# Feed-forward of a decoder layer: four fp32 matmuls per chunk become eight float32r matmuls on a split input

## The chip, the cores and the metric

The kernel runs on one core of one Trainium2 chip. A core has TensorE (PE, with its weight loads shown apart as PEld), VectorE (DVE), ScalarE (ACT), GpSimd (POOL) and SyncE (SP, which issues the DMAs here). The metric is device time in microseconds, the median over runs. A "pass" below is one record of a matmul in the trace: one stream of columns through the array.

## The reference

One decoder layer over x of shape (2, 2048, 512), in fp32, with three residual blocks:

```python
x = x + attn(layernorm(x), Wq, Wk, Wv, Wo)      # 16 heads of 32, rotary positions, softmax over 2048 keys
x = x + gelu(layernorm(x) @ ctx.T) @ ctx        # ctx: 77 rows of 512
w = (weights >= 0.0) * 2.0 - 1.0                # signs, 512 x 512
x = x + clip((layernorm(x) @ w.T) * scale + bias, -100, 100)
```

The change concerns the third block: its weights are only +1 and -1, and its input is a normalised chunk of 128 rows.

## The kernel before, in words

**Stages.** For each of the two batches, `project_batch` normalises 16 chunks of 128 rows, turns them and makes queries, keys and values; then `Attention.run` goes through 32 units (a block of queries, a group of four heads, a half of 256 queries) of 8 steps each. A step treats 2 x 128 keys for four heads; it has two half-steps, one for each pair of heads. In a half-step TensorE makes scores (`st`, L496, and at times the row maxima's start, L481), the products from which later row maxima are taken (`ps`, L403), the weighted values of the step before (`acc`, L514) and sums of weights (L528); ScalarE takes exponentials (`pw`, L623), VectorE reduces `ps` to maxima (`mx`, L415), GpSimd adds weights up (`sm`, L625).

**The rest of the layer in the gaps.** When all heads of a block of queries are done, `divide` appends `after_attention` for that block to `queue`. It is a generator of small pieces: the output projection (`po`, L309), a layernorm, the two matmuls with ctx (`ph`, L316, and `po`, L335), a layernorm, and the feed-forward (`pf`, L343) with scale, bias, clip and residual, for each chunk of 128 rows. `background(1)` runs one piece of the first generator in the queue. Each `yield` says whether the next piece is heavy (it has matmuls): in the second half-step of every step any piece may run, in the first half-step of every second step only a light one; in the last four units of a batch each half-step may take any piece.

**Order.** Inside `run` the order on PE, DVE, ACT and POOL is that of the program (`tc.manual_schedule`); outside it the framework schedules. Pieces that are left when a batch ends go into the next batch's projection or, after the second batch, into a loop at the end in which `side()` moves the element-wise work from GpSimd to VectorE.

**Buffers.** While attention runs, `bank` gives the background its PSUM banks from `ps_s`, which has three; the `ps` products use two of them in each half-step. Tiles with the tag "w" in `work` (five buffers) hold `xn2`, `h`, `u`, `y` and `num`. The pool `big` has three buffers with the tag "s", which hold `r` in the projection and `pw` in attention.

**The lines around the change.** `norm` (L291) makes `xn2` on ScalarE (L297), transposes it on TensorE into `pt2` (L303; the trace calls it `pt`) and copies it with ScalarE into `ot` (L304), which is the block's own part of the query tile (`q` in the trace). After the layernorm of all n chunks of a block, a loop (L340 to L353) makes, for each chunk, the matmuls

```python
nc.tensor.matmul(pf, ot[:, i, cols], wf[:, i, :], start=(i == 0), stop=(i == ND - 1))
```

and `nc.vector.tensor_mul(y, pf, fs)` (L345); then, a piece each, the addition of the bias (L347), and clip and residual (L349, L350) with the DMA to the output (L352). `late_loads` loads the weights `wf` after the first projection's code and turns them into signs in place (L111, L112).

Of the kernel before, what the change touches and what calls it, by code (L numbers as in the profile page):

```python
# [8 lines left out]

F32 = mybir.dt.float32  # L10
BF16 = mybir.dt.bfloat16
AF = mybir.ActivationFunctionType
ALU = mybir.AluOpType
AX = mybir.AxisListType

P = 128
B, S, D = 2, 2048, 512
H, DK = 16, 32
C = 77
ND = D // P  # L20
BLK = 512
# [9 lines left out]
MAX_VAL = 100.0  # L31
# [4 lines left out]
def decoder_layer(  # L36
# [16 lines left out]
    nc = tc.nc  # L53

    const = ctx.enter_context(tc.tile_pool(name="const", bufs=1))
    kvq = ctx.enter_context(tc.tile_pool(name="kvq", bufs=1))
    xpool = ctx.enter_context(tc.tile_pool(name="xpool", bufs=6))
    big = ctx.enter_context(tc.tile_pool(name="big", bufs=3))
    sums = ctx.enter_context(tc.tile_pool(name="sums", bufs=3))
    work = ctx.enter_context(tc.tile_pool(name="work", bufs=5))  # L60
# [6 lines left out]
    def load_x(b, ch):  # L67
        t = xpool.tile([P, D], F32, tag="x", name=f"x_{b}_{ch}")
        nc.sync.dma_start(t, x[b, ch * P : (ch + 1) * P, :])
        return t  # L70

    def load_w(src, name):
        t = const.tile([P, ND, D], F32, tag=name, name=name)
        nc.sync.dma_start(t, src.rearrange("(i p) o -> p i o", p=P))
        return t


    def load_qkv():
        return [load_w(w, name) for w, name in ((wk_t, "wk"), (wq_t, "wq"), (wv_t, "wv"))]

    x_next = [load_x(0, 0), load_x(0, 1)]
    qkv = load_qkv()
    cos = const.tile([P, NCH, DK // 2], F32, tag="cos", name="cos")
    sin = const.tile([P, NCH, DK // 2], F32, tag="sin", name="sin")
    nc.sync.dma_start(cos, rope_cos.rearrange("(c p) d -> p c d", p=P))
    nc.sync.dma_start(sin, rope_sin.rearrange("(c p) d -> p c d", p=P))

    ident = const.tile([P, P], F32, tag="ident", name="ident")
    make_identity(nc, ident)
    ident_b = const.tile([P, P], BF16, tag="ident_b", name="ident_b")  # L90
    nc.vector.tensor_copy(ident_b, ident)
    ones_b = const.tile([P, P], BF16, tag="ones_b", name="ones_b")
    nc.vector.memset(ones_b, 1.0)
    ones = const.tile([P, DK], F32, tag="ones", name="ones")
    nc.vector.memset(ones, 1.0)
# [5 lines left out]
    for n in range(2):  # L101
        mt = const.tile([P, 2, 4, DK], BF16, tag=f"mt{n}", name=f"mt{n}")
        nc.vector.memset(mt, 0.0)
# [3 lines left out]

    def late_loads():
        late["wo"] = load_w(wo_t, "wo")
        wf = load_w(wf_t, "wf")  # L110
        nc.vector.tensor_scalar(wf, wf, 0.0, 2.0, ALU.is_ge, ALU.mult)  # L111
        nc.vector.tensor_scalar_add(wf, wf, -1.0)  # L112
        late["wf"] = wf
        for name, src in (("fs", f_scale), ("fb", f_bias)):
            t = const.tile([P, D], F32, tag=name, name=name)
            nc.sync.dma_start(t, src.to_broadcast([P, D]))
            late[name] = t
# [9 lines left out]
    def chunk_stats(xc, mv):  # L127
        st = small.tile([P, 6], F32, tag="st", name="st")
        nc.vector.bn_stats(st, xc)
        nc.vector.bn_aggr(mv, st)  # L130


    def scale_and_shift(engine, mv, n):
        y = small.tile([P, n], F32, tag=f"rstd{n}", name="rstd")
        engine.tensor_scalar(y, mv[:, :, 1], EPS, None, ALU.add)
        nc.gpsimd.tensor_tensor(y, y, minus_half[:, :n], ALU.pow)
        off = small.tile([P, n], F32, tag=f"off{n}", name="off")
        engine.tensor_mul(off, mv[:, :, 0], y)
        engine.tensor_scalar(off, off, -1.0, None, ALU.mult)
        return y, off  # L140
# [116 lines left out]
    def side():  # L257
        return nc.vector if alone else nc.gpsimd
# [5 lines left out]
    def bank(shape, name):  # L264
        banks[0] += 1
        if attending or (alone and banks[0] % 2):
            return ps_s.tile(shape, F32, tag="s", name=name)
        return ps_t.tile(shape, F32, tag="t", name=name)


    def after_attention(b, blk, ot, first, end):
        wo, wf, fs, fb = late["wo"], late["wf"], late["fs"], late["fb"]
        ctxn, ctxt = late["ctx"]
        n = end - first
        chunks = [slice(c * P, (c + 1) * P) for c in range(first, end)]
        whole = slice(first * P, end * P)
        xs = [load_x(b, blk * CPB + c) for c in range(first, end)]
        yield True


        def add_to_x(matmuls, mv):
            for c in range(n):
                ps = bank([P, D], "po")
                matmuls(ps, chunks[c])
                nc.vector.tensor_add(xs[c], ps, xs[c])
                yield False
                chunk_stats(xs[c], mv[:, c, :])
                yield c + 1 < n


        def norm(mv):  # L291
            y, off = scale_and_shift(side(), mv, n)
            yield False
            yield False
            for c in range(n):
                xn = work.tile([P, D], F32, tag="w", name="xn2")
                nc.scalar.activation(  # L297
                    xn, xs[c], AF.Identity, bias=off[:, c : c + 1], scale=y[:, c : c + 1]
                )
                yield True  # L300
                pt = bank([P, ND, P], "pt2")
                for i in range(ND):
                    nc.tensor.transpose(pt[:, i, :], xn[:, i * P : (i + 1) * P], ident)  # L303
                nc.scalar.copy(ot[:, :, chunks[c]], pt)  # L304
                yield c + 1 == n

        def project_out(ps, cols):
            for i in range(ND):
                nc.tensor.matmul(ps, ot[:, i, cols], wo[:, i, :], start=(i == 0), stop=(i == ND - 1))  # L309

        mv = small.tile([P, n, 2], F32, tag=f"mv{n}", name="mv2")
        yield from add_to_x(project_out, mv)
        yield from norm(mv)
        ph = bank([C, n * P], "ph")
        for i in range(ND):
            nc.tensor.matmul(ph, ctxt[:, i, :], ot[:, i, whole], start=(i == 0), stop=(i == ND - 1))  # L316
        h = work.tile([C, n * P], F32, tag="w", name="h")
        nc.scalar.copy(h, ph)
        yield False
        u = work.tile([C, n * P], F32, tag="w", name="u")  # L320
        side().tensor_mul(u, h, h)
        yield False
        side().tensor_scalar(u, u, 0.044715, 1.0, ALU.mult, ALU.add)
        side().tensor_mul(u, u, h)
        yield False
        yield False
        nc.scalar.activation(u, u, AF.Tanh, scale=GELU_C)
        yield False
        side().tensor_scalar(u, u, 1.0, 0.5, ALU.add, ALU.mult)
        side().tensor_mul(u, u, h)  # L330
        yield False
        yield True

        def attend_ctx(ps, cols):
            nc.tensor.matmul(ps, u[:, cols.start - whole.start : cols.stop - whole.start], ctxn, start=True, stop=True)  # L335

        mv = small.tile([P, n, 2], F32, tag=f"mv{n}", name="mv3")
        yield from add_to_x(attend_ctx, mv)
        yield from norm(mv)
        for c, cols in enumerate(chunks):  # L340
            pf = bank([P, D], "pf")
            for i in range(ND):
                nc.tensor.matmul(pf, ot[:, i, cols], wf[:, i, :], start=(i == 0), stop=(i == ND - 1))  # L343
            y = work.tile([P, D], F32, tag="w", name="y")
            nc.vector.tensor_mul(y, pf, fs)  # L345
            yield False
            side().tensor_add(y, y, fb)  # L347
            yield False
            side().tensor_scalar(y, y, -MAX_VAL, MAX_VAL, ALU.max, ALU.min)  # L349
            side().tensor_add(xs[c], xs[c], y)  # L350
            r0 = blk * BLK + (first + c) * P
            nc.sync.dma_start(out[b, r0 : r0 + P, :], xs[c])  # L352
            yield True  # L353

# [20 lines left out]
    class Attention:  # L377
# [53 lines left out]
        def turn_maxima(self, u):  # L431
            mt = mts[u % 2]
            mrow = small.tile([P, 2, P], BF16, tag="mrow", name="mrow")
            if u > 0:
                nc.sync.dma_start_transpose(mrow, mt.rearrange("p c h d -> p (c h d)"))
            else:
                pt = ps_s.tile([P, 2, P], BF16, tag="s", name="ptm")
                for c in range(2):
# [213 lines left out]
    for b in range(B):  # L652
        att = Attention(b)
        project_batch(b, x_next, att, *qkv)
        if b == 0:
            late_loads()
        load_ctx(b)
        att.run()
        if b + 1 < B:
            x_next = [load_x(b + 1, 0), load_x(b + 1, 1)]  # L660
            qkv = load_qkv()
# [51 lines left out]
```

## Time and profile before

| | us |
|---|---|
| median of 3 runs (lowest, highest) | 2783.71 (2783.66, 2784.01) |
| the profiled execution's own time | 2784.56 |
| its span, from first to last instruction | 2782.8 |
| PE busy | 2750.7 (99%) |
| PEld, weight loads, overlapping PE | 1491.3 (54%) |
| POOL busy | 1756.4 (63%) |
| DVE busy | 1675.7 (60%) |
| ACT busy | 1320.4 (47%) |
| mean granted TensorE clock | 0.996 |

Busy times overlap between engines. A PE that is busy all the time is not at its peak, since ends of matmuls are modelled; start times are what can be relied on. In the groups of instructions, the numbers after the bar are busy us in total and mean ns of one, then idle time of the engine just before them with what ended it. In the timeline, the first two columns are start and length in us.

### The profile page before, as it was taken

The page shows a single profiled execution, that of the slowest core. Times are in us where ns is not written, and L with a number is a line of the kernel's source. Part 1 is how long each engine was busy: PE and PEld are TensorE (multiplying, and loading weights), DVE is VectorE, ACT ScalarE, POOL GpSimd, SP SyncE. Part 2 cuts the span into 40 slices and gives each one's busy share as a digit, 9 for nine tenths or more (in the row PEclk, how much of TensorE's full clock was granted, in tenths as well). Part 3 has the DMA queues.
Part 4 walks back from the last instruction along what each step waited for, and adds up shares of the span by engine and source line. Part 5 has one row for each costly group of instructions (what it writes and reads, how often), then busy time and mean ns, then how long its engine had stood idle before and what let it go on. Part 6 is the DMA issues. An engine that isn't in the chain of part 4 may idle for free.

```text
span 2782.8 us, 70154 instructions
## 1 busy us (share of the span) xinstructions
PE 2750.7 (99%) x30748; PEld 1491.3 (54%) x30748; DVE 1675.7 (60%) x2792; ACT 1320.4 (47%) x2391; POOL 1756.4 (63%) x1903
## 2 busy tenths in 40 slices
PE   8999999999999999999999999999999999999997
PEld 4445555555555555555444455555555555555554
DVE  3436777676666666665234367766757666666652
ACT  2114555455545554654321155555555455545552
POOL 3226767567756685777542277766777567756764
PEclk9999999999999999999999999999999999999999
DMA  4000000000000000000210000000000000000000
GB/s 141 19 16 2 5 4 4 4 4 19 19 4 4 10 27 3 4 19 18 69 31 27 15 4 4 4 4 4 4 24 14 4 4 15 22 3 4 22 7 16
DMA packets 41858, 43.52 MB, mean 16 GB/s; under 512 B 24758, under 2 KB 24758, under 8 KB 41552
## 3 DMA queue, kind: packets, MB, share of 16 engines
q1 hardware_dynamic: 41552, 39.05, 4.7%
q8 instruction: 240, 3.93, 0.6%
q14 instruction: 66, 0.54, 0.1%
HBM read 26.58 MB, written 8.39 MB: 13 GB/s over the span
## 4 chain that ended last, share of the span: by engine, by line
PE 97%; POOL 1%; DVE 1%; DMA 0%; ACT 0%; issue 0%; ACTq 0%; POOLq 0%; DVEq 0%
PE st L496 22%; PE acc L514 22%; PE ps L403 18%; PE acc L528 8%; PE po L309 4%; PE pf L343 4%; PE pq L168 4%; PE pk L168 4%; PE pv L168 4%; PE st L481 3%; PE pt L303 1%; PE po L335 1%; PE ph L316 1%; PE ptqk L176 1%; PE pt L161 1%
## 5 line engine op out<-in xcount | busy, mean ns | idle before, releaser
L625 POOL TENSOR_TENSOR sm<-pw 128x512 f32<-128x512 f32 x1024 | 1296.6, 1271 | 634.5 <-ACT pw L623 631.8
L415 DVE TENSOR_REDUCE mx<-ps 128x1 f32<-128x512 f32 x2048 | 1310.3, 681 | 582.0 <-PE ps L403 579.5
L623 ACT ACTIVATE pw<-st 128x512 f32<-128x512 f32 x2048 | 1111.8, 595 | 1001.8 <-PE ps L403 668.8
L403 PE MATMUL ps<-k,q 32*128 32x512 f32 x4096 | 1208.8, 640 | 1.6 <-DVE mx L415 1.6
L514 PE MATMUL acc<-pw,v 128*32 128x256 f32 x8192 | 655.6, 391 | 0.0
L528 PE MATMUL acc<-sm,ones 128*32 128x128 f32 x7680 | 389.0, 280 | 0.0
L403 PEld LDWEIGHTS ps<-k,q 32*128 32x128 f32 x4096 | 355.3, 183 | 37.7 <-issue 25.8
L514 PEld LDWEIGHTS acc<-pw,v 128*32 128x32 f32 x8192 | 162.4, 108 | 396.3 <-issue 376.6
L528 PEld LDWEIGHTS acc<-sm,ones 128*32 128x32 f32 x7680 | 247.4, 110 | 153.9
L496 PE MATMUL st<-q,dkk 32*128 32x256 f32 x2048 | 291.1, 400 | 0.0
L496 PE MATMUL st<-q,dkq 32*128 32x256 f32 x2048 | 289.9, 400 | 0.0
L496 PE MATMUL st<-q,dkv 32*128 32x256 f32 x2048 | 289.9, 400 | 0.0
L496 PE MATMUL st<-q,k 32*128 32x256 f32 x2048 | 262.8, 374 | 0.0
L201 POOL TENSOR_TENSOR r<-r 128x512 f32<-128x512 f32 x64 | 82.1, 1282 | 246.6 <-DVE r L200 246.3
L496 PEld LDWEIGHTS st<-q,dkk 32*128 32x128 f32 x2048 | 175.4, 184 | 93.2 <-issue 52.3
L496 PEld LDWEIGHTS st<-q,dkq 32*128 32x128 f32 x2048 | 172.7, 184 | 82.6 <-issue 56.7
L496 PEld LDWEIGHTS st<-q,dkv 32*128 32x128 f32 x2048 | 174.7, 184 | 65.2 <-issue 33.6
L496 PEld LDWEIGHTS st<-q,k 32*128 32x128 f32 x2048 | 195.2, 187 | 14.2
L548 DVE RECIPROCAL num<-num 128x128 f32<-128x128 f32 x128 | 120.2, 941 | 60.8 <-ACT num L542 60.8
L177 ACT COPY q<-ptqk 128x512 f32<-128x512 f32 x32 | 18.8, 587 | 232.5 <-PE ptqk L176 232.5
L168 PE MATMUL pk<-wk,xnt 128*128 128x512 f32 x256 | 120.7, 615 | 2.7 <-ACT xnt L163 2.7
L168 PE MATMUL pq<-wq,xnt 128*128 128x512 f32 x256 | 120.9, 612 | 0.0
(90 smaller groups left out, 1860.7 us busy)
## 6 DMA issues: line engine op xcount, KB each, us to landing
x<-in_x_dram SPq DMA_DIRECT2D x64, 256.0 KB, 2.7
out_dram<-x SPq DMA_DIRECT2D x32, 256.0 KB, 2.0
wk<-in_wk_t_dram SPq DMA_DIRECT2D x2, 1024.0 KB, 5.5
wq<-in_wq_t_dram SPq DMA_DIRECT2D x2, 1024.0 KB, 10.5
wv<-in_wv_t_dram SPq DMA_DIRECT2D x2, 1024.0 KB, 9.7
wo<-in_wo_t_dram SPq DMA_DIRECT2D x1, 1024.0 KB
wf<-in_wf_t_dram SPq DMA_DIRECT2D x1, 1024.0 KB, 9.8
mrow<-mt SPq DMA_TRANSPOSE x62, 2.3
```

The source lines that it names most:

```text
L168: nc.tensor.matmul(dst, xnt[:, i, :], w[:, i, :], start=(i == 0), stop=(i == ND - 1))
L309: nc.tensor.matmul(ps, ot[:, i, cols], wo[:, i, :], start=(i == 0), stop=(i == ND - 1))
L343: nc.tensor.matmul(pf, ot[:, i, cols], wf[:, i, :], start=(i == 0), stop=(i == ND - 1))
L403: nc.tensor.matmul(ps, self.q[qb][self.rows[h], g, q0 : q0 + P], self.k[kb][self.rows[h], g, :], start=True, stop=True,)
L415: nc.vector.tensor_reduce(mx[:, qc, h, kb : kb + 1], ps, AX.X, ALU.max)
L481: nc.tensor.matmul(self.st[h], ones_b[r, :], mrow[r, None, :].to_broadcast([DK, 2, HQ]), start=True, stop=False, skip_group_check=True,)
L496: nc.tensor.matmul(self.st[h][:, c, :], keys[r, g, kc * P : (kc + 1) * P], self.q[qb][r, g, hf * HQ : (hf + 1) * HQ], start=False, stop=Tr ...
L514: nc.tensor.matmul(acc[self.rows[h], 0, :], self.v[self.chunk(i, c)][:, d0 : d0 + DK], pw[:, h, c, :], start=(i == 0 and c == 0), stop=(i ...
L528: nc.tensor.matmul(acc[self.rows[h], 1, part], ones, sm[:, h, part], start=False, stop=(i == STEPS - 1), skip_group_check=True,)
L548: nc.vector.reciprocal(num[:, 1, part], num[:, 1, part])
L623: nc.scalar.activation(pw[:, h], self.st[h], AF.Exp, scale=SCALE)
L625: nc.gpsimd.tensor_add(sm[:, hs, :], pw[:, hs, 0, :], pw[:, hs, 1, :])
```

## The change

The feed-forward's matmuls are made in float32r, a 4-byte type with a shorter mantissa; as the change has it, such a matmul is one pass where an fp32 one is two. The signs are exact in it. The normalised, transposed chunk is split into two parts: `high` is `pt2` written as float32r (ScalarE[...]), `low` is `pt2 - high` (VectorE). Four matmuls with `high` and four with `low` are accumulated in `pf`. The feed-forward of a chunk now follows its own transposes, in `norm`, by the argument `take`, in place of a loop after all chunks; the number of pieces, and of heavy ones, is the same. `ot` is not written by the second layernorm any more. The weights are loaded into a buffer of `big`, and their signs written into a float32r tile.

```diff
 def late_loads():
     late["wo"] = load_w(wo_t, "wo")
-    wf = load_w(wf_t, "wf")
-    nc.vector.tensor_scalar(wf, wf, 0.0, 2.0, ALU.is_ge, ALU.mult)
-    nc.vector.tensor_scalar_add(wf, wf, -1.0)
+    drawn = big.tile([P, ND, D], F32, tag="s", name="wf")
+    nc.sync.dma_start(drawn, wf_t.rearrange("(i p) o -> p i o", p=P))
+    nc.vector.tensor_scalar(drawn, drawn, 0.0, 2.0, ALU.is_ge, ALU.mult)
+    wf = const.tile([P, ND, D], F32R, tag="wf", name="signs")
+    nc.vector.tensor_scalar_add(wf, drawn, -1.0)
     late["wf"] = wf
...
-        def norm(mv):
+        def norm(mv, take):
...
-                nc.scalar.copy(ot[:, :, chunks[c]], pt)
-                yield c + 1 == n
+                yield from take(c, pt)
+
+        def keep(c, pt):
+            nc.scalar.copy(ot[:, :, chunks[c]], pt)
+            yield c + 1 == n
+
+        def feed_forward(c, pt):
+            parts = [work.tile([P, ND, P], F32R, tag="w", name=name) for name in ("high", "low")]
+            nc.scalar.copy(parts[0], pt)
+            nc.vector.tensor_sub(parts[1], pt, parts[0])
+            yield True
+            pf = bank([P, D], "pf")
+            for k, part in enumerate(parts):
+                for i in range(ND):
+                    nc.tensor.matmul(
+                        pf,
+                        part[:, i, :],
+                        wf[:, i, :],
+                        start=(k == 0 and i == 0),
+                        stop=(k == 1 and i == ND - 1),
+                    )
+            y = work.tile([P, D], F32, tag="w", name="y")
+            nc.vector.tensor_mul(y, pf, fs)
+            yield False
+            side().tensor_add(y, y, fb)
+            yield False
+            side().tensor_scalar(y, y, -MAX_VAL, MAX_VAL, ALU.max, ALU.min)
+            side().tensor_add(xs[c], xs[c], y)
+            r0 = blk * BLK + (first + c) * P
+            nc.sync.dma_start(out[b, r0 : r0 + P, :], xs[c])
+            yield False
...
-        yield from norm(mv)
+        yield from norm(mv, keep)
...
-        yield from norm(mv)
-        for c, cols in enumerate(chunks):
-            pf = bank([P, D], "pf")
-            for i in range(ND):
-                nc.tensor.matmul(pf, ot[:, i, cols], wf[:, i, :], start=(i == 0), stop=(i == ND - 1))
-            y = work.tile([P, D], F32, tag="w", name="y")
-            nc.vector.tensor_mul(y, pf, fs)
-            yield False
-            side().tensor_add(y, y, fb)
-            yield False
-            side().tensor_scalar(y, y, -MAX_VAL, MAX_VAL, ALU.max, ALU.min)
-            side().tensor_add(xs[c], xs[c], y)
-            r0 = blk * BLK + (first + c) * P
-            nc.sync.dma_start(out[b, r0 : r0 + P, :], xs[c])
-            yield True
+        yield from norm(mv, feed_forward)
```

## The prediction

> **What bounds the kernel now.** I read the page's busy times and its chain of waits first.
>
> ```profile
> PE 2750.7 (99%) x30748; PEld 1491.3 (54%) x30748; DVE 1675.7 (60%) x2792; ACT 1320.4 (47%) x2391; POOL 1756.4 (63%) x1903
> ...
> PE 97%; POOL 1%; DVE 1%; DMA 0%; ACT 0%; issue 0%; ACTq 0%; POOLq 0%; DVEq 0%
> PE st L496 22%; PE acc L514 22%; PE ps L403 18%; PE acc L528 8%; PE po L309 4%; PE pf L343 4%; PE pq L168 4%; PE pk L168 4%; PE pv L168 4%; PE st L481 3%; PE pt L303 1%; PE po L335 1%; PE ph L316 1%; PE ptqk L176 1%; PE pt L161 1%
> ```
>
> The end is set by TensorE nearly throughout, and `pf`, the line that changes, holds 4% of the chain. Since a busy PE need not be a bound, I then looked in the timeline at start times around one `pf`:
>
> ```profile
> 664.15 0.64 PE L514 MATMUL acc<-pw,v 128*32 128x256 f32 x8
> ...
> 664.93 3.70 PE L343 MATMUL pf<-wf,q 128*128 128x512 f32 x8
> ...
> 669.63 0.64 PE L514 MATMUL acc<-pw,v 128*32 128x256 f32 x8
> ...
> 671.53 0.64 PE L514 MATMUL acc<-pw,v 128*32 128x256 f32 x8
> ```
>
> From L514 to L514 is one half-step: 5.48 us with `pf`, 1.90 us without. So `pf` costs 3.6 us of progress, its full length on PE, and nothing else hides it. Half-steps without `ps` (the last units) take 1.85, those with it 1.86 to 1.90: PE's own stream sets the pace, VectorE's maxima are just short of it. The groups by shape give the durations:
>
> ```profile
> L343 PE MATMUL pf<-wf,q 128*128 128x512 f32 x256 | 119.8, 612 | 0.0
> L349 POOL TENSOR_SCALAR y<-y 128x512 f32<-128x512 f32 x30 | 57.6, 1921 | 0.2
> L285 DVE TENSOR_TENSOR x<-po,x 128x512 f32<-128x512 f32 x64 | 43.7, 685 | 102.8 <-PE po L309 89.6 <-PE po L335 13.2
> L304 ACT COPY q<-pt 128x512 f32<-128x512 f32 x64 | 37.5, 586 | 13.9 <-PE pt L303 13.2
> L303 PEld LDWEIGHTS pt<-ident,xn 128*128 128x128 f32 x256 | 27.5, 143 | 27.0 <-ACT xn L297 12.1 <-ACT pw L623 7.8 <-issue 7.1
> ```
>
> 256 records for 32 x 4 matmuls: two passes each. The chain has eight passes of 512 columns in 3.43 us in the projection, 0.429 each; in attention a group costs 3.60, so 0.17 is the price of changing over, which stays.
>
> **What the Trainium skill says.** "Perfetto Trace Analysis", Engine Utilization: the array gives 307.2 G elements/s, half of it for FP32_LOW_HIGH. For 128 x 512 that is 0.213 and 0.427 us; the trace's fp32 pass, 0.429, is the halved one. "FP8 and Floating Point Precision", TensorE Precision Notes: the array is natively about FP22, "FP32 reduced precision" reads 4 bytes and truncates to FP22, and true fp32 takes four passes. The trace shows two passes of half rate, which is the same time. No rate is stated for the reduced form. "TensorE: Matmul & The Clock Gate", Wait — 56ns, not 53.3ns?: a warm pass of 512 columns measures 0.2157 us. The one kind here that isn't fp32 agrees: `st` by L481 in bf16, 512 columns, is followed on the same rows after 0.23 us.
>
> ```profile
> 637.94 0.39 PE L481 MATMUL st<-mrow,ones_b 32*128 32x512 bf16 x2
> ...
> 638.17 0.59 PE L496 MATMUL st<-q,k 32*128 32x256 f32 x4
> ```
>
> **The change, part by part.**
>
> The passes. Per chunk, 8 x 0.429 = 3.43 us go; 8 float32r passes of 512 columns come, and no float32r is in the trace. Lower bound 0.2157 (the rate of a non-fp32 pass), upper 0.429 (4-byte data at fp32's rate). I take 0.2157: the halving is named for the two-part form alone, and a one-part operand leaves no reason for it. Weight loads of 4-byte data, 128 x 128, must then fit under 0.2157: the transposes, a load and a 128-column pass each, run four in 0.59 us, 0.147 apart, so loads at that pace fit. Gain: 8 x (0.429 − 0.2157) = 1.706 us a chunk.
>
> Where the chunks are. The compiled order keeps all 28 chunks inside attention, two in the second batch's projection and two in the last loop, and the last `pf` of each block falls in the same half-step as before; `pf` follows its transposes by two half-steps (one in the last units). 28 x 1.706 = −47.8. In the projection PE is bound as well: 2 x 1.706 = −3.4.
>
> The last loop. PE has been idle and is cold: the skill's clock page ("What's actually happening") gives half clock after an idle window, and the trace shows the first eight passes there taking 5.3 us (2768.4 to 2773.7), the next eight 3.4, so cold lasts to about 2772.1. With short passes: `high` is there at 2768.2, eight cold passes (0.43 each) end at 2771.7, then one cold and seven warm at 2773.7. On DVE `low` (0.69, twice) lies under this; after the second `pf` its chain of 0.69 + 0.69 + 0.43 + 0.69, mixed with one addition of the first chunk, ends near 2777.1, before 2779.8: −2.5.
>
> The split. ScalarE's copy to `high` replaces the copy to `ot`, 0.586 for 0.586: 0. `tensor_sub` is new on DVE, nearest row L285 (PSUM and SBUF in, 128x512), 0.685 x 32 = 21.9 us busy, DVE at 60%. Behind it on DVE stand the reductions of the next half-step, and for these PE waits by its three PSUM banks. The copy ends 2.07 us after the L514 of the half-step of the transposes (2.45 to 2.56 long), so the subtraction lies from 2.1 to 2.8, 0.3 us into the next, where reductions are due at 0.1. The trace has the like: BATCH_NORM_STATS2 (0.69) at 597.64 pushes the reductions from 0.10 to 0.23 and that half-step takes 1.99 instead of 1.90; where they are pushed to 0.45 it takes 2.21. Bounds 0.1 and 0.31; I take 0.18 x 28 = +5.0. `pf` itself does not wait: it comes at least a half-step later.
>
> GpSimd. Bias, clip and residual (1.27 + 1.92 + 1.27 = 4.46) are the same work, spread over chunks, but less PE time covers them. In the last units the cycle becomes five half-steps: 5 x 1.9 + 0.59 + 1.9 = 12.0 us, in which POOL has 5 x 1.27 + 4.46 plus about 0.6 of `divide` and maxima = 11.4. Before: three half-steps with `pf`, 9.3 us against 8.7. After a clip, `sm` lags 3.2 to 3.5 us already now (4.5 once) and PE doesn't wait; the sums are used about two half-steps later. I take +1.5 in all, from 0 to 10.
>
> The signs. `drawn` takes the buffer of `r` of chunk 13, free when its transposes end at 201.6; on SP it comes behind x loads already issued by 189.3. 1 MB lands 5.5 to 9.8 us later (times of L74), 207 to 211.4. On DVE it stands between two copies of keys with 2.7 us idle (208.5 to 211.2), before `ps` reductions at 213.2. Between 0 and +4; I take +1.0. On SP the maxima's transposes behind it aren't due until later units. The two operations' cover in the first chunks falls away, 2.4 us that nobody waited for.
>
> Other edits (two `take` functions, `keep`) change no instruction: 0. "w" gets two more tiles per chunk, but their readers end before five more are taken: 0.
>
> Sum: −47.8 − 3.4 − 2.5 + 5.0 + 1.5 + 1.0 = −46.2. The profiled execution's 2784.6 (span 2782.8 and 1.8 around it) would become 2738.4; the median is 0.85 below that execution, so 2737.5.
>
> **The rivals.**
>
> R1, half rate: float32r streams at fp32's 0.429 because of its four bytes. For it: every 4-byte matmul in the trace has this rate, and no page states another. Against it: the name in the halving rule. Then the passes gain nothing and the additions remain: 2783.7 + 5.0 + 1.5 + 1.0 + 0.7 (`low` in the last loop) = 2792, slower. It decides from a pass of about 0.40 us upwards, where 30 x 8 x (0.429 − p) equals the 7.5 of costs.
>
> R2, weight loads not hidden: the array can't start a load under so short a pass, and pass plus load make 0.30 (0.2157 and the part of 0.147 that is left). For it: PEld rows show 0.19 for these loads; against it: the loads of `pf` now idle 0.24 between, so they run ahead. Gain 30 x 8 x 0.129 = 31, time 2783.7 − 31 − 2 + 7.5 = 2758.
>
> R3, another engine takes over around `pf`: GpSimd's 11.4 of 12.0, or the reductions with the subtraction ahead of them. If each of 28 chunks loses 0.5 us more, 2751.5. Against it: the lags above that cost nothing.
>
> **How the numbers follow.** Chances: forecast 0.76, R1 0.11, R2 0.06, R3 0.07. With its bounds (subtraction −2 to +4, signs −1 to +3, GpSimd −1.5 to +8, not all at once) the forecast's own range is 2729 to 2747. R3 and half of R2 reach to 2757; so 2727 to 2757 leaves R1, the rest of R2 and the forecast's edges out, 0.2. A measurement tells 0.2%, 5.6 us, from no change: faster 0.89 (forecast, R2, R3), slower 0.08 and same 0.03 (R1, whose 2792 has the bound at 2789.3 below it).
>
> **What would show it.** Right: `pf` with 256 records in float32r, eight of them in about 1.73 us by starts, a half-step with `pf` at 3.8 us instead of 5.5; the half-step after the transposes 0.1 to 0.3 longer; span near 2736. Wrong: starts 0.43 apart (R1), 0.3 (R2), PE idle before L528 by `sm` or L403 by `mx` (R3); a stall near 208 to 214 by `drawn`. More than two records per pair of parts and slice would make the change itself untrue.

## The result

The changed kernel takes 2735.1 us (median of 4 runs, 2733.57 to 2737.15) against 2783.7 before: a ratio of 0.9827, 95% interval 0.9813 to 0.9841. The forecast was 2737.5, range 2727 to 2757. On a third chip, later, it took 2736.4 against 2783.9, ratio 0.9831 (0.9818 to 0.9844). The total is close to the forecast; its terms are less so, and two misses of 4 to 5 us stand against each other, as the next sections show.

The page of the changed kernel, busy times and the chain of waits:

```profile
PE 2700.9 (99%) x30748; PEld 1493.1 (55%) x30748; DVE 1695.3 (62%) x2824; ACT 1321.0 (48%) x2391; POOL 1755.2 (64%) x1903
...
PE 98%; DVE 1%; POOL 0%; ACT 0%; issue 0%; DMA 0%; ACTq 0%; POOLq 0%
PE st L516 22%; PE acc L534 22%; PE ps L423 18%; PE acc L548 8%; PE po L343 4%; PE pq L171 4%; PE pk L171 4%; PE pv L171 4%; PE st L501 3%; PE pf L323 2%; PE pt L306 1%; PE po L369 1%; PE ph L350 1%; PE ptqk L179 1%; PE pt L164 1%
```

The bound is where it was. PE is busy 49.8 us less with as many records (30748: per chunk, two for each of four matmuls before, one for each of eight now), and `pf` went from 4% of the chain to 2%. VectorE has 32 instructions and 20 us more.

The timeline around one `pf` of the changed kernel, and its groups by shape (count, then busy us and mean ns, then idle time before):

```profile
640.58 0.64 PE L534 MATMUL acc<-pw,v 128*32 128x256 f32 x8
...
641.36 1.19 PE L323 MATMUL pf<-signs,high 128*128 128x512 f32 x4
...
642.39 1.09 PE L323 MATMUL pf<-signs,low 128*128 128x512 f32 x4
...
644.49 0.64 PE L534 MATMUL acc<-pw,v 128*32 128x256 f32 x8
```

```profile
L323 PE MATMUL pf<-signs,high 128*128 128x512 f32 x128 | 39.4, 431 | 0.1
L323 PE MATMUL pf<-signs,low 128*128 128x512 f32 x128 | 36.0, 403 | 0.0
...
L318 DVE TENSOR_TENSOR low<-pt,high 128x512 fp32r<-128x512 f32 x32 | 22.0, 687 | 48.2 <-ACT high L317 48.2
...
L317 ACT CAST high<-pt 128x512 fp32r<-128x512 f32 x32 | 18.8, 586 | 14.6 <-PE pt L306 14.6
```

From L534 to L534 a half-step with `pf` is now 3.91 us where it was 5.48. Its passes start 0.23 us apart, not 0.429 and not the 0.2157 of the forecast: from the first start to what follows `pf` it is 2.06 us in each of the 28 groups of attention within 0.02, against 3.63. The mean durations of 431 and 403 ns would mislead here, since the records overlap: they start 0.23 us apart and are 0.39 us long or more. The split costs what it was costed at on its engines, 0.687 and 0.586 us.

Where the 49.2 us between the two profiled executions (spans of 2782.8 and 2733.6) went, by stages cut at the first and last weighted-value matmuls of each batch:

| stage | before, us | after, us | difference |
|---|---|---|---|
| first projection, to the first L514 or L534 | 228.26 | 229.68 | +1.42 |
| attention of batch 0 | 1133.44 | 1112.20 | −21.24 |
| second projection | 249.51 | 242.67 | −6.84 |
| attention of batch 1 | 1132.39 | 1111.13 | −21.25 |
| last loop | 39.20 | 37.90 | −1.29 |

Only the two attention stages repeat: in a second profile of the changed kernel (r1_changed below) they are 1112.25 and 1111.31, while its first projection is 231.9 and its last loop 35.1. What moves the other stages is taken up below.

### The profile page after: what moved, and what is told of

Read it like the earlier page. It is cut to its first block, busy times and chain, and to the rows that moved or that the text cites. A ratio compares the mean times of both kernels' runs of the same rounds, so it can differ in the third digit from the quotient of the medians.

```text
span 2733.6 us, 70216 instructions
## 1 busy us (share of the span) xinstructions
PE 2700.9 (99%) x30748; PEld 1493.1 (55%) x30748; DVE 1695.3 (62%) x2824; ACT 1321.0 (48%) x2391; POOL 1755.2 (64%) x1903
## 4 chain that ended last, share of the span: by engine, by line
PE 98%; DVE 1%; POOL 0%; ACT 0%; issue 0%; DMA 0%; ACTq 0%; POOLq 0%
PE st L516 22%; PE acc L534 22%; PE ps L423 18%; PE acc L548 8%; PE po L343 4%; PE pq L171 4%; PE pk L171 4%; PE pv L171 4%; PE st L501 3%; PE pf L323 2%; PE pt L306 1%; PE po L369 1%; PE ph L350 1%; PE ptqk L179 1%; PE pt L164 1%
## 5 line engine op out<-in xcount | busy, mean ns | idle before, releaser
L534 PE MATMUL acc<-pw,v 128*32 128x256 f32 x8192 | 655.6, 391 | 0.0
L534 PEld LDWEIGHTS acc<-pw,v 128*32 128x32 f32 x8192 | 162.5, 108 | 396.9 <-issue 378.6
```

The source lines that it names most:

```text
L534: nc.tensor.matmul(acc[self.rows[h], 0, :], self.v[self.chunk(i, c)][:, d0 : d0 + DK], pw[:, h, c, :], start=(i == 0 and c == 0), stop=(i ...
```

## The experiments

Two theories stood from the start. T: the gain is the shorter pass of float32r and little else. O: the new order, feed-forward right behind each chunk's transposes, carries a good part of it. The two misses to be explained were the pass (0.232 for 0.2157) and the subtraction (free, where the forecast had 5 us). e1 to e4 ran on a second chip, where the kernel before takes 2783.1 us; the others on the third, where it takes 2783.9.

**e1_order_fp32: the order alone.**

```diff
-            parts = [work.tile([P, ND, P], F32R, tag="w", name=name) for name in ("high", "low")]
+            parts = [work.tile([P, ND, P], F32, tag="w", name="whole")]
             nc.scalar.copy(parts[0], pt)
-            nc.vector.tensor_sub(parts[1], pt, parts[0])
```

(and the signs loaded and made as in the kernel before; `stop` goes to the last matmul that is left, here and in e2)

> The order of the changed kernel (feed-forward of each chunk right after its transposes), but fp32: no split, four two-pass matmuls, signs made in place early. Theory (the gain is the shorter pass): a pf group costs 3.63 us again, attention takes 1133.4 us per batch as before, the first L514-type matmul starts at 228.3 us as before, and only the stall in the second batch's projection can go, 2 to 5 us: 2779 to 2782 us. Rival (the order itself carries a good part of the gain, by spreading the work over half-steps): 2770 us or less. Rival (the projection's stall comes from the length of the passes, not from their place): 2783.7 us.

Measured: 2782.9 us, ratio to before 0.9999 (0.9991 to 1.0007). The timeline of this kernel:

```profile
639.17 0.64 PE L531 MATMUL acc<-pw,v 128*32 128x256 f32 x8
...
639.96 3.70 PE L320 MATMUL pf<-wf,whole 128*128 128x512 f32 x8
...
644.66 0.64 PE L531 MATMUL acc<-pw,v 128*32 128x256 f32 x8
```

A half-step with `pf` is 5.49 us again. O falls: the order is worth nothing in the median. The median is 0.9 us above the theory's range and 0.8 below the second rival, while single executions reach from 2779.8 to 2786.1, so it does not decide between these two. Attention is 1134.24 and 1133.18 us, 0.8 longer per batch than before: some half-steps with moved pieces are 0.1 longer. In the profiled execution the second projection was 242.8 us, as short as the changed kernel's, and yet the median has no gain. So that part of the difference comes and goes with the execution; the section on the hardware says with what.

**e2_high_only: half of the passes, no subtraction.**

```diff
-            parts = [work.tile([P, ND, P], F32R, tag="w", name=name) for name in ("high", "low")]
+            parts = [work.tile([P, ND, P], F32R, tag="w", name="high")]
             nc.scalar.copy(parts[0], pt)
-            nc.vector.tensor_sub(parts[1], pt, parts[0])
```

> Leaves out the low part: no subtraction on VectorE, four float32r passes per chunk in place of eight. Theory (a pass costs 0.232 us of progress, the subtraction about 0.05): 28 x (0.93 + 0.05) + 2 x 0.93 + about 1 at the end = 30 us less than the changed kernel, about 2705 us. Rival (a group has a large fixed cost, so half of the passes save less): 2715 us or more. Rival (the subtraction costs the 0.18 of the forecast): 2701 us.

Measured, with the low part's products left out: 2706.7 us, ratio 0.9727 (0.9714 to 0.9740), as the theory had it within 2 us. Its executions reach from 2702.3 to 2709.7, so the median rules out the large fixed cost but not the 2701 of the last rival; the stages do that. A group is 1.13 us long in place of 2.06, so four passes are 0.93 and a fixed 0.20 is left. Attention of batch 0 is 1099.68, 12.5 us less than in the changed kernel; the passes alone make 14 x 0.93 = 13.0. With 0.18 for each subtraction it would be 15.5. Nothing is left for the subtraction.

**e3_cols256: the same columns in twice as many passes and weight loads.**

```diff
-            for k, part in enumerate(parts):
-                for i in range(ND):
-                    nc.tensor.matmul(pf, part[:, i, :], wf[:, i, :], ...)
+            for o in (slice(0, D // 2), slice(D // 2, D)):
+                for k, part in enumerate(parts):
+                    for i in range(ND):
+                        nc.tensor.matmul(pf[:, o], part[:, i, :], wf[:, i, o], ...)
```

> Each float32r matmul cut in two of 256 columns: sixteen passes and sixteen weight loads per chunk, same product. Theory A (a pass is its columns at 2.4 per ns plus about 19 ns): 16 x (0.107 + 0.019) + 0.1 = 2.1 us per group, about 2735 to 2737 us in all. Theory B (0.232 us is the pace of loading 128 x 128 4-byte weights, whatever the columns): 16 x 0.232 + 0.1 = 3.8 us per group, 1.75 x 30 = 52 us more than the changed kernel, 2787 us.

Measured: 2734.9 us, ratio 0.9831 (0.9818 to 0.9845), the same as the changed kernel. Four passes of 256 columns start every 0.47 us:

```profile
925.17 0.63 PE L324 MATMUL pf<-signs,low 128*128 128x256 f32 x4
925.64 0.63 PE L324 MATMUL pf<-signs,high 128*128 128x256 f32 x4
926.11 0.63 PE L324 MATMUL pf<-signs,low 128*128 128x256 f32 x4
```

That is 0.117 each, half of 0.232. Theory B falls: loading 128 x 128 4-byte weights fits under 0.117 us. Theory A had the total right and the reason wrong: with a fixed 19 ns per pass it would be 0.126. The time goes with the columns, 512 in 0.232 or 256 in 0.117, 2.2 columns per ns.

**e4_bf16_parts: another type.** Two bf16 parts keep some 16 bits of each value, fewer than two float32r parts, so this is not the same product.

```diff
-        wf = const.tile([P, ND, D], F32R, tag="wf", name="signs")
+        wf = const.tile([P, ND, D], BF16, tag="wf", name="signs")
...
-            parts = [work.tile([P, ND, P], F32R, tag="w", name=name) for name in ("high", "low")]
+            parts = [work.tile([P, ND, P], BF16, tag="w", name=name) for name in ("high", "low")]
```

> Both parts and the signs in bf16 in place of float32r, all else the same[...]. If the 0.232 us of a pass comes from 4-byte operands (their weight load), a bf16 pass is 0.216 and 30 x 8 x 0.016 = 4 us go: 2731 us. If it is the cost of changing weights with every pass in any type: 2735 us. If bf16 weights load slower or VectorE writes them slower, more than 2736 us.

Measured: 2727.2 us, ratio 0.9804 (0.9791 to 0.9817). From `high` to `low` four passes take 0.87 us (one record of each group is missing from this trace):

```profile
641.22 1.04 PE L323 MATMUL pf<-signs,high 128*128 128x512 bf16 x3
642.09 1.03 PE L323 MATMUL pf<-signs,low 128*128 128x512 bf16 x4
```

The passes start 0.216 apart, the forecast's own number, so the 8% on each pass belongs to float32r. The half-step with `pf` is 0.22 us shorter, of which 8 x 0.016 = 0.13 are the passes; the rest lies at the first pass, which in float32r is followed 0.33 to 0.34 us later, 0.1 more than its successors (`high` to `low` was 1.03 us there), and in bf16 is not. The gain of 8 us was twice what was expected, since only the passes had been counted.

**e6_two_subs and e6_three_subs: where VectorE begins to bind.** The subtraction is made again, to the same tile:

```diff
             nc.vector.tensor_sub(parts[1], pt, parts[0])
+            nc.vector.tensor_sub(parts[1], pt, parts[0])
```

> The subtraction on VectorE made twice, to the same tile. Theory (VectorE has some 0.6 us to spare in each half-step, so the first one cost next to nothing and the second begins to push PE's banks): the half-steps after the transposes 0.1 to 0.5 us longer, 28 x 0.3 = 8 us, 2743 us. Rival (each subtraction costs the 0.18 of the forecast, linearly): 5 us more, 2740 us, and the first one's 5 us are hidden somewhere in the other terms. Rival (VectorE is nowhere near): 2735 us.

> The subtraction made three times. Theory (spare time used up): every further 0.69 us lands on PE in full or nearly so, 28 x 0.6 = 17 us more than with two, about 2760 us. Rival (linear 0.18): 2745 us. Rival (VectorE nowhere near): 2736 us.

Measured: 2746.8 us with two (ratio 0.9873, 0.9859 to 0.9886) and 2763.9 with three (0.9930, 0.9917 to 0.9944), beside 2736.4 for the changed kernel on the same chip (r1_changed). So one costs nothing, the second 10 us and the third 17: not linear, and the theory's numbers within 4 us. The attention stages, which repeat, give 13.4 and 17.8. The same half-step after the transposes shows why. In the changed kernel (from L534 at 638.57 to L534 at 640.58, 2.01 us):

```profile
637.50 0.59 ACT L317 CAST high<-pt 128x512 fp32r<-128x512 f32 x1 [0.24 <-PE pt L306]
...
638.18 0.69 DVE L318 TENSOR_TENSOR low<-pt,high 128x512 fp32r<-128x512 f32 x1 [0.82 <-ACT high L317]
638.57 0.64 PE L534 MATMUL acc<-pw,v 128*32 128x256 f32 x8
...
638.79 1.28 DVE L435 TENSOR_REDUCE mx<-ps 128x1 f32<-128x512 f32 x2
...
640.58 0.64 PE L534 MATMUL acc<-pw,v 128*32 128x256 f32 x8
```

and with two subtractions (638.55 to 641.28, 2.73 us):

```profile
638.55 0.64 PE L535 MATMUL acc<-pw,v 128*32 128x256 f32 x8
...
638.89 0.69 DVE L319 TENSOR_TENSOR low<-pt,high 128x512 fp32r<-128x512 f32 x1
...
639.50 2.65 DVE L436 TENSOR_REDUCE mx<-ps 128x1 f32<-128x512 f32 x4
...
641.28 0.64 PE L535 MATMUL acc<-pw,v 128*32 128x256 f32 x8
```

The usual half-step of this kind is 1.97. With one subtraction the reductions of the maxima start 0.22 us after L534, right behind it, and PE loses 0.03 us; with two they start at 0.95, and PE loses another 0.72. In e1, without a subtraction, they start at 0.00 in such half-steps. So PE bears a delay of some 0.2 us at this place, and what goes beyond it lands on PE in full. It is so in 16 of the 28 half-steps after transposes, where the second subtraction costs 0.69 to 0.73; in eight others it costs 0.3 to 0.5, and in the last four, without `ps`, nothing.

**r1_changed and e7_bf16_early: the signs made early again, with bf16 parts.**

```diff
-        drawn = big.tile([P, ND, D], F32, tag="s", name="wf")
...
+        wf = const.tile([P, ND, D], BF16, tag="wf", name="signs")
+        for i in range(0, ND, 2):
+            drawn = const.tile([P, 2, D], F32, tag="drawn", name="wf")
+            nc.sync.dma_start(drawn, rows[:, i : i + 2, :])
+            nc.vector.tensor_scalar(drawn, drawn, 0.0, 2.0, ALU.is_ge, ALU.mult)
+            nc.vector.tensor_scalar_add(wf[:, i : i + 2, :], drawn, -1.0)
```

> The changed kernel again, on the chip of the three runs beside it, so that these can be set against it: 2734 to 2737 us.

> Parts and signs in bf16 as in e4_bf16_parts (the chunk carried in 16 bits), and the weights loaded in two halves into a tile of their own, which is free from the start, so that the signs are made early. Theory (the late signs cost 1.4 us at the last chunk of the first projection): first L514-type matmul at 228.3 us in place of 229.5, in all 8 us less than the changed kernel for the passes and 1.3 for the signs: 2726 us. Rival (the two waiting loads on SP hold up the x loads behind them): 2728 us or more.

Measured: 2736.4 us for r1_changed, as expected, and for e7_bf16_early 2726.7 us (2726.26 to 2727.91), ratio 0.9798 (0.9784 to 0.9811), 9.7 us under the changed kernel on the same chip and the shortest that carries two parts. The first L514-type matmul came at 229.3, not 228.3, but for another reason than the signs made late: the first projection ran 1.0 us later from its second chunk on (`pk` at 23.70, before at 22.68). The changed kernel has the same in its first profile (23.61) and not in its second (22.55), so it varies between executions; whether the two early loads add to it, as the rival has it, stays open. From the last chunk's `pk` to the first L501-type matmul it is 203.76 to 225.11, 21.35 us, as in the kernel before (202.74 to 224.09); with the late signs it is 21.85 (203.66 to 225.51). So the late signs cost 0.5 us in their own place. That is also all that separates the medians of e7 and e4, on two chips, and it is less than the noise.

## Why the prediction was right, step by step

- **The bound.** Right: PE's stream sets the pace, and what is taken from `pf` is gained in full. Attention of e1, 1134.24, less 14 x 1.57 is 1112.2, which is what the changed kernel takes.
- **The passes, −47.8 in attention.** The mechanism was right, the size off. The group went from 3.63 to 2.06 us: 28 x 1.57 = −44.0. The mis-sized term is the pass, taken as 0.2157, the rate of a pass that isn't fp32; float32r takes 0.232. The changeover stayed, as the forecast had it, at 0.20 us (3.63 − 3.43, and 2.06 − 1.86) where it had read 0.17. The upper bound of 0.429 (R1) is out.
- **The subtraction, +5.0.** Wrong. The step that failed is the price taken from the half-step beside BATCH_NORM_STATS2. The push came as forecast: in four half-steps the reductions start 0.22 us after L534, there 0.23, and the half-step takes 2.00, there 1.99. But that one is of a kind that takes 1.90 undisturbed, while 16 of the 28 half-steps after transposes hold L501 as well and take 1.97 in any case. So four lose 0.03 us and twelve, where the reductions start at 0.15, nothing; in the other twelve the next half-step has `pf` ahead of its `ps`, or no `ps`, and lost nothing either. e2 and the e6 pair show that the first 0.69 us was spare and the next was not. With two subtractions, 1.4 us, about a third of the added VectorE time landed on PE (13.4 of 38 us).
- **GpSimd, +1.5.** The size fits, by another path. No wait of PE for `sm` appears in the changed kernel, though the sums lag up to 4.6 us behind their exponentials (at 1225.73). 2 x 0.8 us were lost, but e1, with fp32, loses them as well: it is the order. Which of its neighbours costs them was not followed further.
- **The second projection, −3.4.** −6.8. The passes give 2.9 (3.44 and 3.54 before, 2.06 and 2.04 now). Most of the rest is a wait and TensorE's clock: in the profile of before this happened, and in that of after it did not:

```profile
1464.91 1.12 PE L403 MATMUL ps<-k,q 32*128 32x512 f32 x2
...
1465.62 1.38 DVE L129 BATCH_NORM_STATS2 st<-x 128x6 f32<-128x512 f32 x2 [2.11 <-DMA x<-in_x_dram]
1466.91 1.27 DVE L415 TENSOR_REDUCE mx<-ps 128x1 f32<-128x512 f32 x2
1467.64 1.81 PE L403 MATMUL ps<-k,q 32*128 32x512 f32 x2 [1.61 <-DVE mx L415]
...
1469.38 6.36 PE L168 MATMUL pq<-wq,xnt 128*128 128x512 f32 x8
```

PE waited 1.61 us for a reduction that stood behind statistics of an x chunk whose load was late, and then eight passes took 6.2 us by starts where others take 3.4; the clock record has half clock from 1467.94 for 6.83 us. The forecast counted only the passes; what it left out is that such waits and stretches of half clock come and go here. Two profiles without half clock in this stage, e1 with fp32 and e6_three_subs with float32r, take 242.8 and 240.6 us, 2.2 apart, so the passes are about what the change is worth. In the medians the rest counts little, as e1 shows.

- **The signs, +1.0.** 0.5 in their place (21.85 for 21.35), but not by the step's own path. The load was issued at 202.63 and landed 5.1 us later, a little sooner than forecast. L115 was done at 213.97, though, and the reductions began at 215.77 because they waited for `ps`; they did not wait for the signs. What changed is the order of the passes that the framework made: six passes of `pq`, then twelve of `ps`, where with early signs (before, e1, e7) two of `pq` and four of `ps` take turns. PE then waits 0.77 us for a reduction. The other 0.9 of the stage's +1.4 arose between the first and the second chunk, as told under e7, and isn't the signs'. The wait of 0.77 is in all seven profiles with late signs. In one of them, r1_changed, a stretch of half clock follows: eight passes take 5.5 us by starts, and L501 comes 25.15 us after `pk`.

```profile
215.46 2.32 PE L423 MATMUL ps<-k,q 32*128 32x512 f32 x6 [0.77 <-DVE mx L435]
217.71 1.52 PE L171 MATMUL pq<-wq,xnt 128*128 128x512 f32 x2
...
221.17 5.66 PE L171 MATMUL pv<-wv,xnt 128*128 128x512 f32 x8
```

- **The last loop, −2.5.** −1.3 in this profile. At half clock the passes took 0.427 us, as costed (0.43), but half clock held to 30.2 us after the last L534, where the forecast had carried 28.2 over from before. That step was unsafe: in r1_changed, the same kernel, half clock ended 25.7 us after the last L534 and the loop took 35.1 us, −4.1. One profile cannot check this term.

The sum: −44.0 + 1.6 − 6.8 + 1.4 − 1.3 = −49.1 between the two profiles, for −46.2. That it came out 3 us off owes something to luck: the forecast had 3.8 too much gain on the passes and 5.0 too much cost on the subtraction, and these errors cancel; 3.4 more came in the second projection, mostly by the wait and the clock of one execution. None of the rivals came true: R1 (half rate), R2 (loads not hidden) and R3 (another engine) each failed at the point that the forecast named, starts 0.43 or 0.3 apart, or waits for `sm` and `mx`.

## What to carry to other kernels

When one engine sets the pace and a half-step with an operation can be set beside one without it, its worth is the difference of two start times, and a change of its passes can be costed to a few per cent before it is made; the unknown is then the price of the new pass alone, which is worth measuring first. An engine that is 60% busy can still have only one instruction's worth of slack at the place where a new one is put: look at how late its next result may come before the bounding engine waits, not at the share. Where one execution differs from the next by 3 us, compare stages that repeat, not totals. And bf16 parts instead of float32r parts are worth a trial where 16 bits will do: here they gave another 0.3%.

## What the runs showed of the hardware

Float32r passes stream 2.2 columns per ns: 0.232 us for 512, 0.117 for 256, against 0.216 for 512 in bf16 and 0.429 in each of the two passes of fp32. The Trainium skill, "Perfetto Trace Analysis", Engine Utilization, halves the rate for FP32_LOW_HIGH, which agrees with the two passes of 0.429; why a float32r pass is 8% longer than one of bf16 was not found. The last loop narrows it. There, at half clock, four passes take 1.71 us, 0.427 each, in float32r (first two lines, changed kernel) and in bf16 (last two, e4) alike:

```profile
2723.44 1.91 PE L323 MATMUL pf<-signs,low 128*128 128x512 f32 x4
2725.15 1.45 PE L323 MATMUL pf<-signs,high 128*128 128x512 f32 x4
```

```profile
2716.31 1.91 PE L323 MATMUL pf<-signs,low 128*128 128x512 bf16 x4
2718.02 1.27 PE L323 MATMUL pf<-signs,high 128*128 128x512 bf16 x4
```

So float32r's 8% shows at full clock only: halving the clock makes a bf16 pass 1.98 times as long and a float32r pass 1.84 times. The weight loads are not the reason, as e3 showed.

In the clock records of these runs TensorE has full or half clock, and half clock comes in stretches of 3.41, 6.83, 10.24 or 13.65 us, multiples of 3.41 (but for those that the end of a trace cuts off). The Trainium skill, "TensorE: Matmul & The Clock Gate", What's actually happening, gives a free-running window of about 3.4 us, which agrees. It has the clock fall after at least one idle window, while here 6.83 us of half clock followed PE waits of only 1.61 us (before) and 0.77 us (r1_changed), and the measurement decides; what sets a stretch off stays open, since the same wait of 0.77 us had none in six other profiles. The executions of one kernel differ with it: of the kernel before on the second chip, those with a mean granted clock of 0.996 took 2784.4 to 2785.6 us, those with 0.997 took 2780.7 to 2784.5. So a difference of 3 us in a single profile, as in the second projection, need not be the change's.
